# Attention over a paged cache: earlier key loads, value products moved within their slot, weights loaded in pieces, and a new first load of the condition weights

## The chip, the cores and the metric

The kernel runs on one core of a Trainium2 chip. The metric is the device time of the core in microseconds (us), from start to end of one execution; the time before is the median of three runs. A core has TensorE (PE, matrix products, into PSUM), VectorE (DVE), ScalarE (ACT), GpSimd (POOL) and SyncE (SP, which here only issues DMAs). Each takes its instructions in order and waits where an operand or a buffer isn't ready.

## The reference, cut to what matters

64 sequences of 32 tokens with 512 features. Each gets a 32x32 mixing matrix by its condition, then attention with 32 query heads and 8 key heads of 128 features over 512 cached keys, found by a block table, and its 32 new keys.

```python
W = weights[condition]                        # (64, 32, 32)
x = x + einsum('bct,bcd->bdt', x, W)
q = rope(rmsnorm(x @ Wq.T)); k = rope(rmsnorm(x @ Wk.T)); v = x @ Wv.T
kc = k_cache[block_table]; vc = v_cache[block_table]      # 16 pages of 32 rows
scores = einsum('bqhd,bkhd->bhqk', q, concat(kc, k)) * SCALE
scores = where(valid, scores, -1e30)          # a cached row counts below cache_seqlens
o = einsum('bhqk,bkhd->bqhd', softmax(scores), concat(vc, v))
x = x + o @ Wo.T
```

All is float32.

## The kernel before

The work is tiled by steps. A step is four sequences (called batches, 4 x 32 = 128 tokens) and half of the heads (4 key heads, 16 query heads); 16 steps (NT) do the first half of the heads, 16 more the second half, so there are 32. The first half also makes the mixed x and keeps it transposed in memory (`x1t_d`), and stores its part of the output (`acc_d`); the second half loads both again.

Inside a step the main loop goes over 4 batches (`bt`) and 4 key heads (`g`), 16 slots (`slot = bt * GH + g`). Each slot has the scores of one batch and head with its 512 cached keys (`scores`, L527, then the exponential on ScalarE, L535) and the value products of the slot before (`values`, L585). The rest of the work is put in certain slots:

- slot 0: `new_scores`, the scores of the step's new keys (`psn`, L545) and their exponential `pn`; and `x1_a` and `x1_c` of the next step. `x1_c` (L346) multiplies x with the block-diagonal tile `bd` of condition weights and VectorE adds the result to x (L347). In the second half `x1_a` only loads `acc` and `x1t`, and `x1_c` and `x1_b` do nothing.
- slot 1: `new_values(st, 0)`, the value products of the new keys for two heads: four PSUM tiles `pnv` (L569), one a batch, copied by ScalarE to `nv` (L577).
- slot 3: `x1_b` (transposes of the mixed x, L354), `out_proj` of the step before (L474, 32 passes, with VectorE's addition at L481), `new_values(st, 2)`, and in the first steps the angles of later steps (`angles`, L136 to L150).
- slots 4 to 13: projections of the next step (`k_a`, `q_a`, `v_a`), their norm and rotation on VectorE and ScalarE, and the transposes back (`k_b`, `q_b`).
- slots 5 and 6: the store of the step before, the load of x and of the condition weights of the step after next.

`values` of the second head of a pair ends with three VectorE operations: an addition into `nv` (L597), a reciprocal, and the product `o` (L600), which `turn` transposes into `ot` for the output projection. There is one `nv` buffer, so a step's first copies at L577 come after the last `o` of the step before.

Buffers: all PSUM tiles of projections, transposes, `psn`, `pmix`, `pnv` and `pout` share one pool of four (`ps_p`, tag `pp`); one `new_values` takes all four. The scores have two PSUM tiles, the values two.

Keys: `Batch(...)` asks for the keys of a batch (`load_k`, L279): 16 DMAs of 64 KB from SP, one a page, into one of two buffers `k_t`. A buffer is free again when the four copies `kh` (`head_keys`, L520; in the opening on ScalarE, L518) of its batch are made; in the loop they are made one batch ahead of their scores. The request for batch b + 2 stands at the end of batch b's four slots. Values: GpSimd gathers 128 rows at a time (`fetch`, L303) and ScalarE masks them into place (`fill`, L316), ordered behind the last instruction noted in `last["act"]`.

Weights: `load_w` loads 1 MB from SP. The output weights of the first half are loaded in slots 9 to 12 of step 0, those of the second half in slots 12 to 15 of step 16; the k, v and q weights of the second half in slots 11 to 13 of step 14.

The order of SP's and TensorE's instructions is as written; that of the other engines is made by a planner from estimated times, save in the opening (up to `opening.close()`), where all is in written order. DMAs from SP and ScalarE share eight completion semaphores in turn; a DMA waits for the one before it on the same semaphore.

The opening: ScalarE loads the conditions, reads them as registers and issues four loads of 4 KB into `bd`; SP loads x and the weights q 0, k, q 1, q 2 before the first batch's keys. Sixteen `warm` products keep TensorE busy first.

Of the kernel before, what the change touches and what calls it, by code (L numbers as in the profile page):

```python
# [11 lines left out]
F32 = mybir.dt.float32  # L12
# [7 lines left out]
P = 128  # L20
# [35 lines left out]
def cond_resid_paged_attention_kernel(  # L56
# [36 lines left out]
    cond_row = const.tile([1, NT, BT], I32, tag="cond", name="cond_row")  # L93
    lens_sb = const.tile([P, NT], I32, tag="lens", name="lens_sb")
# [90 lines left out]
    def steps_of(exact, pools):  # L185
# [37 lines left out]
        def load_w(kind, hh, g=0):  # L223
            if kind == "q":
                src = wq[:, (hh * QH + g * REP) * D : (hh * QH + (g + 1) * REP) * D]
            elif kind == "o":
                src = wo[(hh * QH + g * REP) * D : (hh * QH + (g + 1) * REP) * D, :]
            else:
                src = (wk if kind == "k" else wv)[:, hh * GH * D : (hh + 1) * GH * D]
            t = wpool.tile(  # L230
                [P, 4, 512], F32, tag=f"w{kind}{g}", name=f"w{kind}{g}_{hh}_{uid}"
            )
            wt[kind, hh, g] = t
            if kind == "o" and not exact:
                src = src.rearrange("(h j p) e -> h p j e", h=REP, p=S)
                for h in range(REP):
                    nc.sync.dma_start(t[h * S : (h + 1) * S, :, :], src[h])
                return
            nc.sync.dma_start(t, src.rearrange("(c p) e -> p c e", p=P))
# [315 lines left out]
        def new_values(st, g0):  # L555


            if g0 == 0:
                st.nv = work.tile(
                    [P, BT, GH, D + 1], F32, tag="nv", name=f"nv_{st.name}", bufs=1  # L560
                )
            pv = [
                ps_p.tile([P, 2, D + 1], F32, tag="pp", name=f"pnv_{st.name}_{g0}_{bt}")
                for bt in range(BT)
            ]
            for i in range(2):
                for bt in range(BT):
                    own = slice(bt * S, (bt + 1) * S)
                    nc.tensor.matmul(  # L569
                        pv[bt][:, i, :],  # L570
                        st.pn[own, g0 + i, :],
                        st.vn[own, g0 + i, :],
                        start=True,
                        stop=True,
                    )
            for bt in range(BT):
                nc.scalar.copy(st.nv[:, bt, g0 : g0 + 2, :], pv[bt])  # L577
# [94 lines left out]
        if not exact:  # L672
            nc.scalar.dma_start(cond_row, cond.rearrange("(i s) t -> s t i", s=S)[0:1])
            nc.gpsimd.dma_start(pages_sb, pages)
            nc.gpsimd.dma_start(norm_w["q"], qn_w.partition_broadcast(P))
            nc.gpsimd.dma_start(norm_w["k"], kn_w.partition_broadcast(P))
# [40 lines left out]
        load_cond_weights(0, nc.scalar, mybir.EngineType.Activation)  # L717
        load_w("k", 0)
        load_w("q", 0, 1)
        load_w("q", 0, 2)  # L720
        batch = Batch(first, 0)
# [17 lines left out]
        angles(0, trig)  # L739
        x1_a(first)  # L740
# [24 lines left out]
        scores(batch, 0)  # L765
        k_b(first)
# [36 lines left out]
        def pieces(st):  # L803
            do = {
                0: (x1_a, x1_c),
                3: (x1_b,),
# [13 lines left out]
        batch, later = later, Batch(first, 2)  # L820
# [13 lines left out]
        for st in steps:  # L834
# [4 lines left out]
            for bt in range(0 if st.n else 1, BT):  # L839
                this = batch  # L840
                for g in range(GH):
# [5 lines left out]
                    if slot == 1:  # L847
                        new_values(st, 0)
                    for piece in fill.get(slot, ()):
                        if isinstance(piece, tuple):  # L850
                            piece[0](ahead, piece[1])
                        else:
                            piece(ahead)
                    if slot == 3:
                        out_proj(steps[st.n - 1])
                        new_values(st, 2)
                        if st.n + 1 < NT // TRIG:
                            tmp = work.tile(
                                [P, 3, TRIG * HD], F32, tag="w1", name=f"trig_{st.n}"
                            )  # L860
# [7 lines left out]
                    if st.n == 0 and 9 <= slot < 13 or st.n == NT and slot >= 12:  # L868
                        load_w("o", st.hh, (slot - 9 if st.n == 0 else slot - 12))
                    if st.t == NT - 2 and st.hh + 1 < NHH:  # L870
                        if slot == 11:
                            load_w("k", st.hh + 1)
                            load_w("v", st.hh + 1)
                        if slot in (12, 13):
                            for i in range(2):
                                load_w("q", st.hh + 1, 2 * (slot - 12) + i)
# [3 lines left out]
                    if valued is not None:  # L880
                        values(*valued)
# [6 lines left out]
                batch, later = later, None  # L888
                n = st.n * BT + bt + 2
                if n < NHH * NT * BT:  # L890
                    later = Batch(steps[n // BT], n % BT)
                    unfilled += [(later, c) for c in range(VC)]
# [78 lines left out]
```

## Time and profile before

| | us |
|---|---|
| median of 3 runs (2278.62 to 2281.65) | 2279.99 |
| the profiled execution | 2282.54 |
| its span | 2280.7 |
| first output projection begins (step 1) | 120.53 |
| from one output projection to the next, first half (190.68 to 260.84) | 70.16 |
| the same, second half (1316.96 to 1385.91) | 68.95 |
| the same, from step 16 to 17 (1171.85 to 1248.10) | 76.25 |

In the slices of the page, TensorE's clock is at nine tenths or more throughout and the DMA engines are 70 to 80% busy in the first two slices (57 us each), 30 to 50% in most others. A matmul row of the timeline is a run of passes; float32 takes two passes a product, and the length of a pass is modelled, so the distance between starts tells more than the busy time. A projection of 8 passes takes 3.44 us, the output projection of 32 takes 13.75 us, the scores or values of one batch and head 0.89 us.

### The profile page before, as it was taken

Reading aid. Unit: us, or ns where it says so; the run is one execution under the profiler, and the core shown is the slowest. Engines: PE = TensorE matmul, PEld = TensorE weight load, DVE = VectorE, ACT = ScalarE, POOL = GpSimd, SP = SyncE. Lnnn points to the kernel's source line nnn. Section 1 sums busy time; section 2 is a strip of 40 time slices with the busy share of each in tenths; the row PEclk is TensorE's granted clock in tenths of the full one; section 3 lists DMA queues with packets and bytes.
Section 4 is the critical chain, followed back from the end, with each engine's and each line's share of the span. In section 5 each row is a group of like instructions: output and inputs, shape, how many; then the busy total and the mean of one; then the engine's idle time right before and its main releaser. Section 6 shows DMA issues by size and latency. Waiting matters only on the chain.

```text
span 2280.7 us, 41860 instructions
## 1 busy us (share of the span) xinstructions
PE 2233.9 (98%) x13590; PEld 1567.2 (69%) x13590; DVE 1075.5 (47%) x2717; ACT 943.2 (41%) x1726; POOL 772.5 (34%) x1005
## 2 busy tenths in 40 slices
PE   7999999999999999999999999999999999999998
PEld 5766677666776667766677766677666777666775
DVE  4544455544454444554444544445434455444452
ACT  3444444444443334443344334444333444333442
POOL 3423333323333233332333323333323343333331
PEclk9999999999999999999999999999999999999999
DMA  7844454344443444445657444544344554344442
GB/s 219 197 132 127 139 149 127 110 131 142 140 134 117 135 135 139 141 121 161 199 152 175 142 129 127 152 139 136 112 135 132 149 148 118 115 137 142 144 134 68
DMA packets 364486, 318.13 MB, mean 139 GB/s; under 512 B 46737, under 2 KB 308881, under 8 KB 364257
## 3 DMA queue, kind: packets, MB, share of 16 engines
q1 hardware_dynamic: 320064, 176.53, 27.1%
q0 software_dynamic: 41136, 134.55, 19.6%
q10 hardware_dynamic: 3056, 4.27, 0.5%
q8 instruction: 110, 1.80, 0.3%
q14 instruction: 120, 0.97, 0.1%
HBM read 302.59 MB, written 12.58 MB: 138 GB/s over the span
## 4 chain that ended last, share of the span: by engine, by line
PE 88%; DMA 5%; DVE 2%; SPq 2%; issue 1%; ACT 1%; another core or an unknown queue 0%; ACTq 0%; POOL 0%; DVEq 0%
PE pout_x L474 19%; PE po_x L585 18%; PE pp_q_x L390 18%; PE ps_x L527 17%; PE pp_v_x L390 5%; PE pp_k_x L390 5%; PE pt_q_x L434 2%; PE pnv_x L569 2%; DMA raw_x<-in_vc_dram,v_row 2%; SPq L279 1%; PE psn_x L545 1%; DMA wo_x<-in_wo_dram 1%; PE pmix_x L346 1%; DMA k_t_x<-in_kt_dram 1%; PE pt_k_x L434 1%
## 5 line engine op out<-in xcount | busy, mean ns | idle before, releaser
L303 POOL DMA_INDIRECT raw_x<-in_vc_dram,v_row x512 | 511.9, 1000 | 679.4 <-ACT v_x L316 612.0
L585 PE MATMUL po_x<-v_x,pr_x 128*128 128x129 f32 x4096 | 550.4, 277 | 3.7 <-ACT pr_x L535 3.7
L527 PE MATMUL ps_x<-qt_x,kh_x 128*128 128x128 f32 x4096 | 544.2, 276 | 6.9 <-DVE kh_x L520 4.6
L585 PEld LDWEIGHTS po_x<-v_x,pr_x 128*128 128x128 f32 x4096 | 504.6, 192 | 51.4 <-issue 38.4
L527 PEld LDWEIGHTS ps_x<-qt_x,kh_x 128*128 128x128 f32 x4096 | 500.9, 193 | 9.5 <-issue 6.8
L390 PE MATMUL pp_q_x<-wq_x,x1t_x 128*128 128x512 f32 x1024 | 460.6, 592 | 0.0
L535 ACT ACTIVATE pr_x<-ps_x 128x512 f32<-128x512 f32 x512 | 304.8, 600 | 376.3 <-PE ps_x L527 325.4
L474 PE MATMUL pout_x<-wo_x,ot_x 128*128 128x512 f32 x1024 | 445.7, 593 | 1.6 <-ACT nv_x L577 1.3
L316 ACT ACTIVATE v_x<-raw_x,valid 128x512 f32<-128x512 f32 x512 | 361.6, 720 | 115.2 <-DMA raw_x<-in_vc_dram,v_row 112.4
L474 PEld LDWEIGHTS pout_x<-wo_x,ot_x 128*128 128x128 f32 x1024 | 192.0, 190 | 231.9 <-issue 228.9
L390 PEld LDWEIGHTS pp_q_x<-wq_x,x1t_x 128*128 128x128 f32 x1024 | 187.2, 190 | 198.5 <-issue 198.2
L520 DVE COPY kh_x<-k_t_x 128x512 f32<-128x512 f32 x506 | 215.3, 428 | 201.4 <-PE ps_x L527 102.2
L577 ACT COPY nv_x<-pnv_x 128x258 f32<-128x258 f32 x256 | 77.3, 389 | 337.2 <-PE pnv_x L569 274.3
L400 ACT ACTIVATE sq_q_x<-pp_q_x 128x512 f32<-128x512 f32 x128 | 76.4, 597 | 299.0 <-issue 133.1
L404 DVE TENSOR_REDUCE ms_q_x<-sq_q_x 128x4 f32<-128x512 f32 x128 | 87.2, 681 | 199.2 <-ACT sq_q_x L400 199.2
L407 POOL TENSOR_TENSOR rs_q_x<-ms_q_x,minus_half 128x4 f32<-128x4 f32 x128 | 132.4, 1035 | 129.6 <-DVE ms_q_x L405 129.5
L379 POOL TENSOR_TENSOR cw_k_x<-norm_k,cos 128x64 f32<-128x64 f32 x32 | 10.1, 315 | 440.3 <-DVE ms_k_x L405 440.3
L597 DVE TENSOR_TENSOR nv_x<-po_x,nv_x 128x258 f32<-128x258 f32 x256 | 107.2, 419 | 104.9 <-PE po_x L585 52.9
L411 DVE TENSOR_TENSOR rope_q_x<-pp_q_x,cw_q_x 128x512 f32<-128x512 f32 x128 | 87.3, 682 | 102.6 <-PE pt_k_x L434 102.6
L390 PE MATMUL pp_v_x<-wv_x,x1t_x 128*128 128x512 f32 x256 | 115.2, 593 | 0.2 <-DMA wv_x<-in_wv_dram 0.2
L390 PE MATMUL pp_k_x<-wk_x,x1t_x 128*128 128x512 f32 x256 | 115.2, 592 | 0.0
L600 DVE TENSOR_TENSOR o_x<-nv_x,rden 128x256 f32<-128x256 f32 x256 | 107.5, 420 | 3.3
(95 smaller groups left out, 1426.0 us busy)
## 6 DMA issues: line engine op xcount, KB each, us to landing
k_t_x<-in_kt_dram SPq DMA_DIRECT2D x2048, 64.0 KB
wq_x<-in_wq_dram SPq DMA_DIRECT2D x8, 1024.0 KB
raw_x<-in_vc_dram,v_row POOLq DMA_INDIRECT x512, 4.3
wo_x<-in_wo_dram SPq DMA_DIRECT2D x32, 256.0 KB
xt_x<-in_x_dram SPq DMA_DIRECT2D x16, 256.0 KB
x1t_d<-x1t_x ACTq DMA_DIRECT2D x16, 256.0 KB
acc_d<-xt_x SPq DMA_DIRECT2D x16, 256.0 KB
acc_x<-acc_d SPq DMA_DIRECT2D x16, 256.0 KB
```

What stands on the lines that cost most here:

```text
L303: nc.gpsimd.indirect_dma_start(out=raw.rearrange("p g d -> p (g d)"), out_offset=None, in_=vc, in_offset=bass.IndirectOffsetOnAxis(ap=v_ro ...
L316: nc.scalar.activation(v_bufs[b % 2][:, c, :, 0:D], raw, AF.Copy, scale=ok)
L390: nc.tensor.matmul(pp, st.x1t[:, c, :], w[:, c, :], start=(c == 0), stop=(c == KC - 1))
L407: nc.gpsimd.tensor_tensor(rs, ms, minus_half, ALU.pow)
L411: nc.vector.tensor_tensor(r.rearrange("p h e f -> p h (e f)"), pp.rearrange("p (h d) -> p h d", h=4), cw.rearrange("p e f -> p (e f)").uns ...
L474: nc.tensor.matmul(po, st.ot[:, i, :], wt["o", st.hh, i // 4][:, i % 4, :], start=(i == 0), stop=(i == QH - 1),)
L520: last["dve"] = nc.vector.tensor_copy(k, ba.k_raw[:, :, g, :]).ins
L527: nc.tensor.matmul(ps[:, c, :], ba.k[g][:, c * P : (c + 1) * P], queries(ba, g), start=True, stop=True,)
L535: last["act"] = nc.scalar.activation(pr, ps, AF.Exp, scale=SCALE).ins
L585: nc.tensor.matmul(ba.po[:, g % 2, :], ba.pr[g][:, c, :], ba.v_t[:, c, g, :], start=(c == 0), stop=(c == VC - 1),)
L597: nc.vector.tensor_tensor(t, ba.po, t, ALU.add)
L600: nc.vector.tensor_tensor(ba.o[:, both, :], t[:, :, 0:D], rd.unsqueeze(2).to_broadcast([P, 2, D]), ALU.mult,)
```

## The change

Five edits. The request for keys moves to the start of a batch's slots. In slots 0 to 3 `values` comes ahead of the pieces; `new_values(st, 2)` stands behind the scores of slot 3, ahead of `values`, `x1_b` and `out_proj`; `x1_c` moves from slot 0 to slot 2; `new_values` notes its last copy in `last["act"]`, behind which `fill` and the angles are ordered. Weights are loaded in halves (`load_parts`), over slots 4 to 11 of steps 0 and 16 and over 12 slots of steps 14 and 15. In the opening the condition weights of step 0 come by one gather of GpSimd and four VectorE copies, and k and q 1 are loaded by GpSimd behind it, the keys ahead of q 2.

```diff
-        def load_w(kind, hh, g=0):
+        def load_w(kind, hh, g=0, part=slice(0, 4), eng=nc.sync):
...
+            if part.start == 0:
+                wt[kind, hh, g] = wpool.tile(
+                    [P, 4, 512], F32, tag=f"w{kind}{g}", name=f"w{kind}{g}_{hh}_{uid}"
+                )
+            t = wt[kind, hh, g]
             if kind == "o" and not exact:
                 src = src.rearrange("(h j p) e -> h p j e", h=REP, p=S)
-                for h in range(REP):
+                for h in range(part.start, part.stop):
                     nc.sync.dma_start(t[h * S : (h + 1) * S, :, :], src[h])
                 return
-            nc.sync.dma_start(t, src.rearrange("(c p) e -> p c e", p=P))
+            eng.dma_start(t[:, part, :], src.rearrange("(c p) e -> p c e", p=P)[:, part, :])
+
+        def load_parts(which, hh, at):
+
+            if 0 <= at < 2 * len(which):
+                load_w(which[at // 2][0], hh, which[at // 2][1], slice(at % 2 * 2, at % 2 * 2 + 2))
...
-                nc.scalar.copy(st.nv[:, bt, g0 : g0 + 2, :], pv[bt])
+                last["act"] = nc.scalar.copy(st.nv[:, bt, g0 : g0 + 2, :], pv[bt]).ins
...
-            nc.scalar.dma_start(cond_row, cond.rearrange("(i s) t -> s t i", s=S)[0:1])
+            nc.scalar.dma_start(cond_0, cond[:, 0:1])
+            nc.vector.tensor_scalar(cond_0, cond_0, float(S), row, ALU.mult, ALU.add)
...
-        load_cond_weights(0, nc.scalar, mybir.EngineType.Activation)
-        load_w("k", 0)
-        load_w("q", 0, 1)
+        w_sel = work.tile([P, S], F32, tag="o", name="w_sel", bufs=1)
+        nc.gpsimd.indirect_dma_start(
+            out=w_sel,
+            out_offset=None,
+            in_=w_cond,
+            in_offset=bass.IndirectOffsetOnAxis(ap=cond_0, axis=0),
+        )
+        nc.scalar.dma_start(cond_row, cond.rearrange("(i s) t -> s t i", s=S)[0:1])
+        load_w("k", 0, eng=nc.gpsimd)
+        load_w("q", 0, 1, eng=nc.gpsimd)
+        batch = Batch(first, 0)
         load_w("q", 0, 2)
-        batch = Batch(first, 0)
...
         angles(0, trig)
+        for i in range(BT):
+            blk = slice(i * S, (i + 1) * S)
+            nc.vector.tensor_copy(bd[blk, blk], w_sel[blk, :])
         x1_a(first)
...
         scores(batch, 0)
+        after = Batch(first, 2)
...
-                0: (x1_a, x1_c),
-                3: (x1_b,),
+                0: (x1_a,),
...
-        batch, later = later, Batch(first, 2)
+        batch, later = later, after
...
             for bt in range(0 if st.n else 1, BT):
-                this = batch
+                this, after = batch, None
+                n = st.n * BT + bt + 2
+                if n < NHH * NT * BT:
+                    after = Batch(steps[n // BT], n % BT)
+                    unfilled += [(after, c) for c in range(VC)]
...
-                    if slot == 1:
-                        new_values(st, 0)
+                    if slot in (1, 3):
+                        new_values(st, slot - 1)
+                    if slot < GH and valued is not None:
+                        values(*valued)
...
+                    if slot == 2 and ahead:
+                        x1_c(ahead)
                     if slot == 3:
+                        if ahead:
+                            x1_b(ahead)
                         out_proj(steps[st.n - 1])
-                        new_values(st, 2)
...
-                    if st.n == 0 and 9 <= slot < 13 or st.n == NT and slot >= 12:
-                        load_w("o", st.hh, (slot - 9 if st.n == 0 else slot - 12))
-                    if st.t == NT - 2 and st.hh + 1 < NHH:
-                        if slot == 11:
-                            load_w("k", st.hh + 1)
-                            load_w("v", st.hh + 1)
-                        if slot in (12, 13):
-                            for i in range(2):
-                                load_w("q", st.hh + 1, 2 * (slot - 12) + i)
+                    if st.t == 0:
+                        load_parts([("o", i) for i in range(GH)], st.hh, slot - GH)
+                    if st.n in (NT - 2, NT - 1):
+                        load_parts(
+                            [("k", 0), ("q", 0), ("q", 1), ("v", 0), ("q", 2), ("q", 3)],
+                            1,
+                            slot - 5 + (st.n - NT + 2) * BT * GH,
+                        )
...
-                    if valued is not None:
+                    if slot >= GH and valued is not None:
                         values(*valued)
...
-                batch, later = later, None
-                n = st.n * BT + bt + 2
-                if n < NHH * NT * BT:
-                    later = Batch(steps[n // BT], n % BT)
-                    unfilled += [(later, c) for c in range(VC)]
+                batch, later = later, after
```

More of the change, by code (lines that the diff above doesn't have):

```diff
@@ L93, in cond_resid_paged_attention_kernel @@
     cond_row = const.tile([1, NT, BT], I32, tag="cond", name="cond_row")
+    cond_0 = const.tile([P, 1], I32, tag="cond_0", name="cond_0")
     lens_sb = const.tile([P, NT], I32, tag="lens", name="lens_sb")
@@ L229, in load_w @@
                 src = (wk if kind == "k" else wv)[:, hh * GH * D : (hh + 1) * GH * D]
[L230 to L233, printed above, removed]
+            if part.start == 0:
[3 more added lines that the diff above has]
+            t = wt[kind, hh, g]
             if kind == "o" and not exact:
                 src = src.rearrange("(h j p) e -> h p j e", h=REP, p=S)
-                for h in range(REP):
+                for h in range(part.start, part.stop):
                     nc.sync.dma_start(t[h * S : (h + 1) * S, :, :], src[h])
                 return
-            nc.sync.dma_start(t, src.rearrange("(c p) e -> p c e", p=P))
+            eng.dma_start(t[:, part, :], src.rearrange("(c p) e -> p c e", p=P)[:, part, :])
+        def load_parts(which, hh, at):
+            if 0 <= at < 2 * len(which):
+                load_w(which[at // 2][0], hh, which[at // 2][1], slice(at % 2 * 2, at % 2 * 2 + 2))
         def load_cond_weights(t, eng=nc.sync, kind=mybir.EngineType.SP):
@@ L853, in steps_of @@
                             piece(ahead)
+                    if slot == 2 and ahead:
+                        x1_c(ahead)
                     if slot == 3:
+                        if ahead:
+                            x1_b(ahead)
                         out_proj(steps[st.n - 1])
-                        new_values(st, 2)
                         if st.n + 1 < NT // TRIG:
-                            tmp = work.tile(
-                                [P, 3, TRIG * HD], F32, tag="w1", name=f"trig_{st.n}"
-                            )
+                            tmp = work.tile([P, 3, TRIG * HD], F32, tag="w1", name=f"trig_{st.n}")
                             with tc.issue_after(last["dve"]), tc.issue_after(last["act"]):
```

## The prediction

> **What bounds the kernel now.** I read the page's busy times first, then TensorE's waits, then the timeline of TensorE over a few steps, then the other engines at the places where it stops.
>
> ```profile
> PE 2233.9 (98%) x13590; PEld 1567.2 (69%) x13590; DVE 1075.5 (47%) x2717; ACT 943.2 (41%) x1726; POOL 772.5 (34%) x1005
> ...
> PE pmix_x L346 <- DMA bd<-in_w_cond_dram: 8.6, 1, 8.6
> PE pnv_x L569 <- DVE xt_x L481: 5.7, 16, 0.4
> PE pnv_x L569 <- DVE acc_x L481: 5.4, 15, 0.4
> PE ps_x L527 <- DVE kh_x L520: 4.6, 1, 4.6
> PE po_x L585 <- ACT pr_x L535: 3.7, 1, 3.7
> ```
>
> TensorE is the bound: 2280.7 - 2233.9 = 46.8 us of the span are not matmul, so no reordering can bring more than that plus what is lost to a slow clock. The wait view (waiter, releaser: total us, times, longest) names four places: the opening, a hole in each of the 31 steps after the first, and two single stops. In the timeline (start us, length us, engine, line, tiles, idle before):
>
> ```profile
> 1798.37 0.73 PE L569 MATMUL pnv_x<-vn_x,pn_x 32*128 32x129 f32 x16
> 1799.03 1.16 PE L585 MATMUL po_x<-v_x,pr_x 128*128 128x129 f32 x8
> ...
> 1816.54 0.50 PE L569 MATMUL pnv_x<-vn_x,pn_x 32*128 32x129 f32 x6
> 1817.39 0.71 PE L569 MATMUL pnv_x<-vn_x,pn_x 32*128 32x129 f32 x10 [0.36 <-DVE acc_x L481]
> 1818.03 1.16 PE L585 MATMUL po_x<-v_x,pr_x 128*128 128x129 f32 x8
> ```
>
> The first half of the new keys' value products takes 1799.03 - 1798.37 = 0.66 us, the second half 1818.03 - 1816.54 = 1.49 us: three products (six passes) run, the fourth waits until the output projection has left the PSUM tile that it needs. That is 0.83 us a step, 31 x 0.83 = 25.7 us, more than the wait view shows (11.1), since pipelined ends are counted busy.
>
> The stops at step changes:
>
> ```profile
> 103.10 1.06 PE L585 MATMUL po_x<-v_x,pr_x 128*128 128x129 f32 x8
> 108.72 2.05 PE L527 MATMUL ps_x<-qt_x,kh_x 128*128 128x128 f32 x8 [4.57 <-DVE kh_x L520]
> ...
> 1233.22 1.08 PE L545 MATMUL psn_x<-qt_x,kn_x 128*32 128x128 f32 x32
> 1237.98 1.16 PE L585 MATMUL po_x<-v_x,pr_x 128*128 128x129 f32 x8 [3.68 <-ACT pr_x L535]
> ```
>
> Both follow the loads of the output weights, 4 MB in a few slots. What else matters is in slots 0 to 3 of an ordinary step:
>
> ```profile
> 749.24 0.43 DVE L520 COPY kh_x<-k_t_x 128x512 f32<-128x512 f32 x1 [2.73 <-DMA k_t_x<-in_kt_dram]
> ...
> 750.23 0.43 DVE L600 TENSOR_TENSOR o_x<-nv_x,rden 128x256 f32<-128x256 f32 x1
> ...
> 750.75 1.21 ACT L577 COPY nv_x<-pnv_x 128x258 f32<-128x258 f32 x4 [2.21 <-DVE o_x L600]
> ...
> SPq L279 <- DVE kh_x L520: 449.6, 60, 11.9
> ```
>
> VectorE stands 2.73 us at a key copy whose keys have not landed; behind it stands the end of the last step's `o_x`, and behind that ScalarE's four copies that empty the first `pnv` tiles, 3.26 us after these products began (747.49). Today nothing on TensorE needs those tiles for a while. The last line says that SP's key loads wait for a free key buffer, not for their place in the queue.
>
> **What the Trainium skill says.** "Perfetto Trace Analysis", Optimizing Tensor Performance, Matmuls: independent groups should rotate through PSUM banks so that emptying one overlaps the next; the trace agrees, and the hole above is this rotation running out (four tiles, all taken by one `new_values`). "TensorE: Matmul & The Clock Gate", HAM oscillation: a TensorE idle for about 3.4 us falls to half clock; here, after 4.57 us, eight score passes take 2.05 us in place of 1.06. "DMA: Bandwidth & Descriptors", Issuing engines are not separate DMA queues: transfers of all queues run on the same 16 engines and interleave; the trace shows the effect, since loads of 8 KB (`lens_sb`) and 4 KB (`bd`) beside the first weights take 5.93 and 8.86 us on the chain of waits. The same page, Anatomy of one DMA, gives about 2.0 us fixed for a GpSimd DMA; the 256 KB gathers here take 4.3 us (median).
>
> **The change, part by part**, against the profiled execution (2282.5 us, span 2280.7; 2.5 above the median).
>
> *Second half of the value products first in slot 3.* Removes the hole: -25.7. It no longer waits for the projection, but for the four copies of the first half, only 7 to 8 us of TensorE work earlier in place of 18. The copies come as late as the keys. In steps with x still to be mixed (first half), `x1_c` moves from slot 0 to slot 2 and needs one of those tiles too, and the second half then needs the tile that VectorE's addition after `x1_c` frees. Worked out from the score product of new keys (`psn`) as zero: the late key copy starts at 5.24 us on average in steps 7 to 14, `o_x` ends 0.97 later, ScalarE's first copy begins at 6.3, and is done after 0.39, the third after 0.93. `x1_c` would be ready at 6.45 (1.01 + 0.99 + 0.99 + 0.66 + 1.0 + 0.89 + 0.9), starts at 6.75 to 7.3: wait 0.3 to 0.85, I take 0.6. The addition behind two key copies, the transpose and the next `o_x` ends near 9.1, about when it is needed: 0.1. So 0.7 in 8 steps: +5.6. In steps 3 to 6 the changed order puts five operations of the angle table (0.23 to 0.29 us each) ahead of that addition, and keys land at 5.6: 1.85 in 4 steps, +7.4. In steps 1, 2, 15 and 17 no late key copy precedes `o_x`, or no mix is left: 0. In the second half (15 steps, no mix): copies from 6.57 to 7.8, the products ready at 7.33 wait 0.27 for the fourth tile; ScalarE's exponentials come after the copies, so the next value products wait some 0.2 more and the projection up to 0.3, against about 0.3 that it waits today: 0.45 net, +6.8. With the mix gone from slot 0, `pn` has 0.9 us less cover in 14 steps, as the second half has today (2.4 us of such waits in the trace): +2. Together -25.7 + 21.8 = -3.9. Ends: the waits could sum to 5 (early tile, keys early) or 40 (last tile, additions late).
>
> *Keys asked for a batch sooner.* The request leaves its place behind the store, the x load and the condition weights (slots 5, 6), so only the fourth batch's keys start about 20 us sooner; they were not late. The batch that stops VectorE in slot 0 is bound by its buffer: copy at 735.78, first load 736.42, 16 loads over some 9 us, landed at 749.24. That stays. In the second half the `acc` and `x1t` loads now stand behind 16 key loads (about 9 us), needed 24 us after slot 0: 0. SP stays behind no new wait: 0, ends -3 and +3.
>
> *Weights in pieces.* Output weights go from slots 9 to 12 of step 0 to slots 4 to 11 as halves, so the keys of step 1 stand behind 2 MB that are done earlier, not 3 MB. The stop at 108.72 should go: 4.57, and the slow clock after it (scores to projection 120.36 - 108.72 = 11.64 against 9.60 elsewhere: 2.0), so -6.6 (ends -3, -7.5). In step 16, 4 MB in slots 12 to 15 become halves in slots 4 to 11; the stop in step 17 costs 1248.10 - 1171.85 = 76.25 us against 68.9 for a neighbour, 7.3; half of the bytes still stand before late keys, I take -5 (0, -7.3). The k, v, q loads of the second half are spread over 12 slots: the 0.85 us wait at 1098 shrinks, -0.5. Cover gone, each would cost what it does now.
>
> *First gather.* The mix waits until 16.61 for condition weights. Now: 512 bytes of indices, one VectorE operation, one gather of 16 KB (issue 1 us, 2 to 4.3 us to land), four small copies that stand behind the angle operations (they end at 13.67 today, since `freq` lands at 11.6). So the mix could start at 10 to 14.2, 2.4 to 6.6 us sooner. But SP's remaining key loads in the opening wait behind ScalarE's DMA of x1t and the four condition loads, on shared semaphores, and wq 2, wv and wq 3 follow those; they would be issued near 23 us, so the third q projection or v becomes late instead. I take -2.5 (ends +1, -7).
>
> Sum: -3.9 - 6.6 - 5.0 - 0.5 - 2.5 = -18.5. 2280.0 - 18.5 = 2261.5.
>
> **Rivals.** *A, the steps gain too*: the tile that `x1_c` gets is free in time, new waits are 0.15 us a step. For it: four tiles and 7 us of cover; against it: the copies at 750.75 lie after the point where `x1_c` would stand. -25.7 + 4.7 - 14.6 = -35.6: 2244. *B, slower*: one mechanism, ScalarE's late first copies. If `x1_c` gets the last tile and the second half waits for an addition behind everything VectorE has queued, a step pays 1.8 us on average, 31 x 1.8 = 56: -25.7 + 56 - 14.6 = +15.5, 2296. It decides from (25.7 + 14.6 + 4.6) / 31 = 1.45 us a step on. For it: VectorE does stand at the keys in nearly all steps; against it: `o_x` to first copy is only 0.09 us, and my sum gives 0.7. *C, the loads only move*: the gains of weights and opening return as late keys (DMA is 70 to 80% busy in the first slices). -3.9 alone: 2276.
>
> **How the numbers follow.** Forecast 0.54, A 0.26, B 0.12, C 0.08. A measurement of this kernel tells 0.2% (4.6 us) from no change. C is half faster, half same; the forecast's own spread puts 0.02 into same. Faster 0.82, same 0.06, slower 0.12. Range 2242 to 2277: from A's gain to C; B is left out with the rest of the tails.
>
> **What would show it.** Right: the wait of `pnv` on the projection's additions is gone, `pmix` and `pnv` wait for ScalarE's `nv` copies or VectorE's addition in the first half, 0.3 to 2 us each, the key copy in slot 0 still waits 2 to 3 us, steps 1 and 17 take 70 us or less to the projection, the first mix starts at 10 to 14 us. Wrong: key copies that no longer wait (then A), waits above 1.45 us a step (B), new stops of 3 us or more behind weight loads (C).

## The result and the profile after

The changed kernel takes 2260.25 us (median of 5 runs, 2257.33 to 2266.80) against 2280.14 us (5 runs, 2278.62 to 2282.26): ratio 0.9916, 95% interval 0.9897 to 0.9935, 19.9 us faster. The profiled execution took 2258.59 us, 23.95 less than the profiled one before. The forecast was 2261.5.

The page's busy times and, below them, the wait view of the kernel after, VectorE's line and then TensorE's (waiter, releaser: total us, times, longest):

```profile
PE 2223.5 (99%) x13590; PEld 1565.7 (69%) x13590; DVE 1076.0 (48%) x2722; ACT 940.4 (42%) x1724; POOL 779.8 (35%) x1008
```

```profile
DVE kh_x L527 <- DMA k_t_x<-in_kt_dram: 68.2, 34, 3.7
```

```profile
PE po_x L592 <- ACT pr_x L542: 5.6, 3, 3.0
PE pp_q_x L397 <- ACT qt_x L469: 3.3, 1, 3.3
PE pmix_x L353 <- DVE bd L757: 2.8, 1, 2.8
...
PE pmix_x L353 <- ACT nv_x L584: 2.2, 3, 1.2
```

TensorE's idle time fell from 46.8 to 2256.8 - 2223.5 = 33.3 us; the other 10 us of the gain were inside what the page counts as busy, as the ends of pipelined products are. The 31 waits of `pnv` on the projection's additions are gone. The late keys are still there: VectorE waits for them 34 times.

The timeline of TensorE in a step of the second half (step 20), from the score product of new keys to the projection:

```profile
1436.05 1.08 PE L552 MATMUL psn_x<-qt_x,kn_x 128*32 128x128 f32 x32
...
1439.05 0.73 PE L576 MATMUL pnv_x<-vn_x,pn_x 32*128 32x129 f32 x16
...
1443.47 0.87 PE L576 MATMUL pnv_x<-vn_x,pn_x 32*128 32x129 f32 x16
...
1445.27 11.32 PE L481 MATMUL pout_x<-wo_x,ot_x 128*128 128x512 f32 x26
```

Both halves of the value products now run through: 0.73 us, and 0.87 with a short pause inside. The same view in the first half (step 3), where x is mixed between them:

```profile
255.17 1.12 PE L353 MATMUL pmix_x<-xt_x,bd 128*128 128x512 f32 x2 [0.53 <-ACT nv_x L584]
256.13 1.05 PE L534 MATMUL ps_x<-qt_x,kh_x 128*128 128x128 f32 x8
257.11 0.50 PE L576 MATMUL pnv_x<-vn_x,pn_x 32*128 32x129 f32 x6
258.49 0.71 PE L576 MATMUL pnv_x<-vn_x,pn_x 32*128 32x129 f32 x10 [0.87 <-DVE xt_x L354]
```

Here are the two new waits of the prediction: the mix behind ScalarE's copy, the fourth value product behind VectorE's addition.

And the chain of waits of the kernel after at step 1, where a stop was forecast to go (start us, length us):

```profile
96.05 9.96 DMA raw_x<-in_vc_dram,v_row
106.06 0.60 issue
106.66 0.58 ACT pr_x L542
...
107.29 1.51 PE po_x L592 x8
```

The stop is still there, and another wait ends it: a gather of values takes 9.96 us from issue to landing, beside the output weights in SP's queue:

```profile
79.56 12.20 SPq L286 DMA_DIRECT2D k_t_x<-in_kt_dram  x16
91.81 5.74 SPq L239 DMA_DIRECT2D wo_x<-in_wo_dram  x8
```

The pieces of slots 8 to 11 stood behind a key request that waited for its buffer until 91.76 us, and then came out as one bunch of 2 MB. Pieces in the program were not pieces in the queue.

The starts of `psn` step by step give the ledger (kernel after less kernel before, in the two profiled executions, us):

| stretch | predicted | measured |
|---|---|---|
| opening, to step 0 | -2.5 | -3.5 |
| step 0 to 2 (output weights, one hole) | -7.4 | +0.3 |
| step 2 to 15 (13 steps, x mixed) | +4.1 | -1.2 |
| step 15 to 18 (weights of the second half) | -7.5 | -5.5 |
| step 18 to 31 (13 steps, no mix) | -4.9 | -13.1 |
| step 31 to end | -0.4 | -0.9 |

Predicted rows are the terms on record, spread over the steps they speak of (one hole of 0.83 beside the -6.6 in the second, 13 of -0.83 + 13.0 + 1.9 in the third, 13 of -0.83 + 0.45 in the fifth). The sum came out; three rows are wrong: the second by 7.7 us one way, the third and the fifth by 5.3 and 8.2 us the other. The pair of profiles differs by 4 us more than the medians do, so a row is not exact. The question for the runs was whether the parts act alone, why the second half gained so much more, and what holds the stop at step 1.

### The profile page after: what moved, and what is told of

Its sections match the earlier page's. It is cut to its first block, busy times and chain, and to the rows that moved or that the text cites. A ratio compares the mean times of both kernels' runs of the same rounds, so it can differ in the third digit from the quotient of the medians.

```text
span 2256.8 us, 41920 instructions
## 1 busy us (share of the span) xinstructions
PE 2223.5 (99%) x13590; PEld 1565.7 (69%) x13590; DVE 1076.0 (48%) x2722; ACT 940.4 (42%) x1724; POOL 779.8 (35%) x1008
## 4 chain that ended last, share of the span: by engine, by line
PE 90%; DMA 4%; DVE 2%; issue 2%; SPq 2%; ACT 1%; POOL 1%; ACTq 0%; DVEq 0%; POOLq 0%
PE pout_x L481 19%; PE pp_q_x L397 19%; PE po_x L592 18%; PE ps_x L534 18%; PE pp_k_x L397 5%; PE pp_v_x L397 5%; PE pt_q_x L441 2%; PE pnv_x L576 2%; DMA raw_x<-in_vc_dram,v_row 2%; SPq L286 1%; PE psn_x L552 1%; DMA k_t_x<-in_kt_dram 1%; PE pt_k_x L441 1%; PE pmix_x L353 1%; DMA pages_at<-in_pages_v_dram 0%
## 5 line engine op out<-in xcount | busy, mean ns | idle before, releaser
L488 DVE TENSOR_TENSOR xt_x<-pout_x,xt_x 128x512 f32<-128x512 f32 x16 | 11.1, 692 | 246.6 <-PE pout_x L481 246.6
L488 DVE TENSOR_TENSOR acc_x<-pout_x,acc_x 128x512 f32<-128x512 f32 x16 | 11.1, 692 | 220.7 <-PE pout_x L481 220.7
```

## The experiments

The kernel before was run beside each group; its median went from 2278.7 to 2283.6 us between groups, so ratios are compared.

### Each part alone

**Slot order (p1).** The edit to the kernel before, with `new_values` noting its last copy as in the change, cut:

```diff
-                0: (x1_a, x1_c),
-                3: (x1_b,),
+                0: (x1_a,),
...
-                    if slot == 1:
-                        new_values(st, 0)
+                    if slot in (1, 3):
+                        new_values(st, slot - 1)
+                    if slot < GH and valued is not None:
+                        values(*valued)
...
+                    if slot == 2 and ahead:
+                        x1_c(ahead)
                     if slot == 3:
+                        if ahead:
+                            x1_b(ahead)
                         out_proj(steps[st.n - 1])
-                        new_values(st, 2)
```

> The kernel before with the slot order alone (second half of the value products first in slot 3, x1_c in slot 2, x1_b in slot 3, value products of slots 0 to 3 ahead of the other pieces). Theory S, the slot order by itself earned what the steps gained in the trace after (2.9 us over steps 2 to 16 and 13.1 us over steps 18 to 31): -14 to -17 us against before, second-half periods at 68.0 to 68.3 us. Rival K, the waits that I charged are real and the earlier key requests removed them: -4 us (my prediction of this part), second-half periods near 68.9 us with waits of pnv on the nv copies of 0.3 us and more.

2274.35 us, ratio 0.9963 (0.9954 to 0.9972), -8.4 us. Its 20 runs spread from 2265.5 to 2280.3; the profiled one is at 2270.96. In that trace the second half gains 13.15 us from step 18 to 31, just what the whole change gains there, with periods of 68.0 to 68.5 us and a few longer ones: theory S holds for the second half, K falls. For the first half S gave -2.9 us, and steps 2 to 15 lose 1.7 us. The last step takes 3.6 us more than before, with a stop of 2.27 us at a key copy. So the time gained less than S gave.

**Keys sooner (p2).**

```diff
-                this = batch
+                this, after = batch, None
+                n = st.n * BT + bt + 2
+                if n < NHH * NT * BT:
+                    after = Batch(steps[n // BT], n % BT)
...
-                batch, later = later, None
+                batch, later = later, after
```

> The kernel before with only the key requests a batch sooner. Theory S and my prediction: 0 us, within 1. Rival K in its strong form (keys sooner shorten every step): -3 us or more, and the key copy of slot 0 starts earlier than 5.2 us after the score product of new keys. If the acc and x1t loads of the second half suffer behind the key loads: +1 to +3 us in steps 17 to 31.

2302.59 us, ratio 1.0081 (1.0055 to 1.0107): 18.5 us slower, which no theory had. The timeline of SP and of TensorE in this kernel:

```profile
66.38 23.55 SPq L279 DMA_DIRECT2D k_t_x<-in_kt_dram  x32
89.98 12.86 SPq L237 DMA_DIRECT2D wo_x<-in_wo_dram  x12
104.12 22.85 SPq L279 DMA_DIRECT2D k_t_x<-in_kt_dram  x16
127.02 1.94 SPq L237 DMA_DIRECT2D wo_x<-in_wo_dram  x4
```

```profile
117.05 10.46 PE L474 MATMUL pout_x<-wo_x,ot_x 128*128 128x512 f32 x24
134.43 6.14 PE L474 MATMUL pout_x<-wo_x,ot_x 128*128 128x512 f32 x8 [6.91 <-DMA wo_x<-in_wo_dram]
```

The last quarter of the output weights stood behind 16 key loads that waited for a buffer until 127 us, and the projection waited 6.91 us for it. Three such stops (13.4 us in the wait view, one in step 1 and two in step 17), one of 4.21 us ahead of the first k projection of the second half, and slow passes after them (8 of the projection take 6.14 us, 24 before them 10.46) make the loss: step 1 to 2 takes 83.67 us in place of 71.20, step 15 to 16 76.14 in place of 69.78, step 17 to 18 82.13 in place of 76.25. Step 0 to 1 is shorter, 44.92 us in place of 50.51. From step 2 to 15 the periods are as before; from step 18 to 31 they sum to 1.6 us more.

**Weights in pieces (p3).**

```diff
-                    if st.n == 0 and 9 <= slot < 13 or st.n == NT and slot >= 12:
-                        load_w("o", st.hh, (slot - 9 if st.n == 0 else slot - 12))
+                    if st.t == 0:
+                        load_parts([("o", i) for i in range(GH)], st.hh, slot - GH)
```

(and `load_parts` for the k, q and v weights, as in the change)

> The kernel before with only the loads of the weights in pieces. My prediction: -12 us (step 0 to 1 -6.6, step 16 to 17 -5.0, step 15 -0.5). Rival C, the stop only moves: as in the trace after, about 0 at step 1 (a late gather beside the output weights instead of late keys) and -3.7 at step 17, -4 us in all. If the new stop of step 1 in the trace after came from the earlier key requests and not from the pieces, the step 0 to 1 period falls to 72 us or less here and the sum is -8 us or better.

2279.15 us, ratio 0.9991 (0.9980 to 1.0003), -2.0 us, with an interval that reaches no change. Step 17 to 18 takes 70.15 us in place of 76.25: that term is right (-6.1). Steps 0 to 2 take 120.6 us in place of 121.7: the stop only moved, to 100.72 us. From its chain of waits:

```profile
81.53 11.77 DMA wo_x<-in_wo_dram
...
96.13 3.13 DMA k_t_x<-in_kt_dram
...
100.72 2.05 PE ps_x L533 x8
```

SP's key loads wait here for the end of an output weight load that takes 11.77 us, and the scores for the late keys. That is not the stop of the kernel after, which a gather ends. So pieces alone don't remove a stop, as rival C says, but whether the one at step 1 depends on the earlier key requests is not told by this run. After an idle time of only 2.29 us TensorE's clock was 0.62 from 100 to 102 us, and eight passes took 2.05 us: a slow clock doesn't need the 3.4 us that the prediction names.

**Opening (p4).**

```diff
-        load_cond_weights(0, nc.scalar, mybir.EngineType.Activation)
-        load_w("k", 0)
-        load_w("q", 0, 1)
-        load_w("q", 0, 2)
-        batch = Batch(first, 0)
+        w_sel = work.tile([P, S], F32, tag="o", name="w_sel", bufs=1)
+        nc.gpsimd.indirect_dma_start(
...
+        load_w("k", 0, eng=nc.gpsimd)
+        load_w("q", 0, 1, eng=nc.gpsimd)
+        batch = Batch(first, 0)
+        load_w("q", 0, 2)
```

> The kernel before with only the opening changed (indices and one gather for the first condition weights, wk and the second wq on GpSimd's queue, cond_row later). My prediction: -2.5 us. The trace after: -3.5 us at the score product of new keys of step 0; the rival is that this head start is lost to late keys or gathers at step 1, because the output weights then meet the same loads: 0 us at the end.

2281.19 us, ratio 0.9990 (0.9978 to 1.0001), -2.3 us; step 0 starts 1.9 us sooner and 2.1 us of it are left at step 14. The size is as predicted, but the interval reaches no change.

The four parts sum to +5.8 us, the change to -19.9: they don't add. The second run suggests which pair interacts: earlier key requests do harm while whole weights stand behind them.

### One part taken out, or moved

**The change without the earlier keys (q1).**

```diff
-                this, after = batch, None
-                n = st.n * BT + bt + 2
-                if n < NHH * NT * BT:
-                    after = Batch(steps[n // BT], n % BT)
-                    unfilled += [(after, c) for c in range(VC)]
+                this = batch
```

(the request goes back to the end of the batch)

> The kernel after with only the key requests back at the end of a batch. The kernel before with the earlier requests alone became 18.5 us slower, since the weights stand behind them in SP's queue. Theory N, with the weights in pieces the earlier requests give nothing (my prediction, 0): within 2 us of the kernel after, some 2260 us, ratio to before 0.991 to 0.992. Theory K, once the pieces are there the earlier requests earn the rest (the sum of the four single parts is +6 us, the change as a whole -19): 8 to 14 us slower than the kernel after, ratio 0.995 to 0.998; step 0 to 1 then takes 49 to 50 us, not 46.6.

2265.78 us, ratio 0.9928 (0.9901 to 0.9955) against 0.9916 (0.9897 to 0.9935) of the whole change: no difference that these runs can tell. Step 0 to 1 does take 50.8 us, not 46.6, but step 1 to 2 then takes 69.5 and not 75.5. Given the other parts, the earlier requests earn about nothing: theory N. The three other parts sum to -12.7 us alone, and this run has -16.4, so most of what doesn't add comes with the key requests. That it is the pieces that keep these from costing 18.5 us is read from the trace of p2; the two were not run together without the rest.

**Half of the first output weights in the opening (q2)**, the rest every second slot.

```diff
         later = Batch(first, 1)
+        load_w("o", 0, 0)
+        load_w("o", 0, 1)
...
-                    if st.t == 0:
+                    if st.n == 0 and slot % 2 == 0:
+                        load_parts([("o", 2), ("o", 3)], st.hh, (slot - GH) // 2)
+                    if st.n == NT:
                         load_parts([("o", i) for i in range(GH)], st.hh, slot - GH)
```

> The kernel after with the first two heads of the first output weights (2 MB) asked for in the opening, behind the second batch's keys, the other two in halves in slots 4, 6, 8 and 10. Theory D, the stop at step 1 is transfer bandwidth (share of the DMA engines 0.94 to 0.98 from 80 to 110 us, 0.44 from 40 to 60 us): steps 0 to 2 take 117 us or less in place of 122.0, ratio to before 0.989 to 0.990. Rival O, it is the order on SP (pieces bunched behind a request that waits for its buffer): the pieces left over still bunch and the stop stays, 121 to 123 us. Rival L, the 2 MB delay q, v and the first gathers in the opening by 2 to 8 us: step 0 starts later by that much and nothing is gained.

2258.60 us, ratio 0.9889 (0.9872 to 0.9905). Steps 0 to 2 take 46.48 + 70.49 = 116.97 us in place of 122.03, the size that theory D gave; step 0 starts 1.9 us later (rival L, in part), and steps 2 to 15 take 3.6 us more than in the kernel after. The view of stretches shows the bytes moved (start:end, length, busy times, clock, DMA share, GB/s). The kernel after:

```profile
40.00:60.00 20.00, 19.39 (x130) 12.33 (x130) 8.77 (x18) 8.52 (x16) 8.47 (x15) 1.00 0.44 128
...
80.00:100.00 20.00, 20.00 (x136) 16.08 (x136) 12.33 (x32) 10.50 (x19) 10.66 (x15) 1.00 0.96 231
```

and this one:

```profile
40.00:60.00 20.00, 19.38 (x112) 11.63 (x111) 9.39 (x19) 10.08 (x19) 9.12 (x15) 1.00 0.79 184
...
80.00:100.00 20.00, 18.98 (x125) 15.03 (x125) 12.93 (x35) 9.60 (x18) 10.65 (x14) 1.00 0.95 223
```

From 80 to 100 us the engines are as full as before, so fullness alone doesn't stop TensorE; what changed is how many weight loads SP issues at once (bunches of four, not eight) and how many fall into these steps. Total and bunching were changed together, and these runs don't separate them.

**The mix back in slot 0 (q3).**

```diff
-                0: (x1_a,),
+                0: (x1_a, x1_c),
...
-                    if slot == 2 and ahead:
-                        x1_c(ahead)
```

> The kernel after with only x1_c back in slot 0, where the kernel before has it; the second half of the value products stays first in slot 3. My prediction put 0.7 to 1.85 us a step of the first half on the tile that x1_c takes in slot 2 (mix behind the nv copies, value products behind the addition). If that term is right, the waits of pmix on nv and of pnv on xt go, and the first-half steps fall from 69.3 to 71.5 us to about 69.4 us: 3 to 8 us faster than the kernel after. Rival: the first value products then find no fourth tile until the addition behind the late keys is done, as in slot 3 of the kernel before: no gain, or a loss of 0.5 us and more in each of 14 steps (+7 us).

2288.31 us, ratio 1.0034 (1.0018 to 1.0050): slower than before the change. The wait view of this kernel, and its timeline in step 7:

```profile
PE pnv_x L576 <- DVE xt_x L354: 20.4, 12, 3.0
```

```profile
536.99 1.02 PE L353 MATMUL pmix_x<-xt_x,bd 128*128 128x512 f32 x2
537.85 1.05 PE L534 MATMUL ps_x<-qt_x,kh_x 128*128 128x128 f32 x8
538.83 0.50 PE L576 MATMUL pnv_x<-vn_x,pn_x 32*128 32x129 f32 x6
542.37 0.71 PE L576 MATMUL pnv_x<-vn_x,pn_x 32*128 32x129 f32 x10 [3.04 <-DVE xt_x L354]
```

The first value products wait for the addition: 1.7 us in each of 12 steps, and steps 2 to 15 take 26 us more than in the kernel after. The main theory of the expectation is wrong, the rival too low. The kernel before mixes in slot 0 too, reaches these products at the same 3.85 us after `psn`, and pays nothing. VectorE's timeline shows why, here:

```profile
541.22 0.43 DVE L527 COPY kh_x<-k_t_x 128x512 f32<-128x512 f32 x1 [3.61 <-DMA k_t_x<-in_kt_dram]
541.57 0.16 DVE L606 RECIPROCAL rden<-nv_x 128x2 f32<-128x2 f32 x1
541.64 0.67 DVE L354 TENSOR_TENSOR xt_x<-pmix_x,xt_x 128x512 f32<-128x512 f32 x1
```

and in the kernel before:

```profile
535.35 0.69 DVE L347 TENSOR_TENSOR xt_x<-pmix_x,xt_x 128x512 f32<-128x512 f32 x1 [3.31 <-PE pmix_x L346]
538.85 0.43 DVE L520 COPY kh_x<-k_t_x 128x512 f32<-128x512 f32 x1 [2.81 <-DMA k_t_x<-in_kt_dram]
```

Since the change emits the value products of slots 0 to 3 ahead of the other pieces, the addition has come to stand behind the late key copy; before, it stood ahead of it. So this run changed two things, and the loss belongs to the place on VectorE's queue. It shows what a place behind the late keys costs, not that slot 0 is bad for the mix.

**The page table first, the second condition weights on SP (q4).**

```diff
+        nc.gpsimd.dma_start(pages_at, pages_v)
...
         load_w("k", 0, eng=nc.gpsimd)
...
-        load_cond_weights(1, nc.scalar, mybir.EngineType.Activation)
+        load_cond_weights(1)
```

> The kernel after with the page and length tables on GpSimd's queue ahead of wk and the second wq, and the condition weights of step 1 on SP in place of ScalarE. If the 8.8 us that the page table takes behind the two weights, and the 6.2 us that ScalarE stands at the condition weights, are what loses the head start (first mix 6.5 us sooner, step 0 only 3.5 us): step 0 starts at 53 to 55 us in place of 56.7, 2 to 4 us faster than the kernel after. Rival: weights then land 0.5 to 1 us later and the q projections wait for these, step 0 within 1 us of 56.7.

2266.70 us, ratio 0.9931 (0.9914 to 0.9948), and step 0 starts 6.4 us later than in the kernel after. The chain of waits shows which half of the edit did it. On SP the small loads came behind the second batch's keys (issued at 40.57 us), and the second mix waited 6.8 us. The first score product had been reached at 32.31 us in place of 34.20, so the page table may be worth its place; the two edits should have been two runs.

### Toward a better version

**The mix behind the value products (s1).** The mix in slot 2 is what still takes a tile between the two halves, so it goes behind them, and the transposes into the projection at three quarters:

```diff
-                    if slot == 2 and ahead:
-                        x1_c(ahead)
                     if slot == 3:
                         if ahead:
-                            x1_b(ahead)
-                        out_proj(steps[st.n - 1])
+                            x1_c(ahead)
+                        out_proj(steps[st.n - 1], ahead and (lambda: x1_b(ahead)))
```

> The kernel after with x1_c moved from slot 2 to slot 3, behind the second half of the value products and ahead of the output projection, and x1_b to three quarters of that projection. Theory T, what the first half still loses is the tile that x1_c takes between the two halves of the value products: the waits of pmix on nv and of pnv on xt go, the first-half steps take 69.3 to 69.6 us each, and steps 2 to 15 take 902 to 905 us in place of 911.3: 6 to 9 us faster than the kernel after, ratio to before 0.987 to 0.989. Rival V, the losses come from VectorE's late keys and angle operations, wherever the mix stands: the addition or the copy of x1t is late for the k projection in slot 4, steps stay at 70 us and more.

2258.94 us, ratio 0.9921 (0.9904 to 0.9937): no faster than the kernel after, yet theory T holds step by step. Steps 2 to 15 take 903.7 us in place of 911.3, most periods are 69.32 us, and the waits on `xt` are gone. The place of the mix and that of the transposes were changed together. The gain is given back in step 1 to 2, 81.97 us in place of 75.47. The chain there:

```profile
127.86 0.45 PE px1t_x L361 x4
128.33 0.59 ACT x1t_x L363
128.95 2.06 DMA x1t_d<-x1t_x
131.02 0.33 SPq L286
```

SP's next key load is released by the end of ScalarE's store of `x1t`. The later transposes make this store later, the keys later, and TensorE waits 6.50 us for a key copy.

**With the earlier output weights (s2).**

> As s1, and 2 MB of the first output weights asked for in the opening, as in q2. If the two gains add: steps 0 to 2 again 117 us in place of 122, 4 to 5 us faster than s1 less up to 2 us in the opening; ratio to before 0.985 to 0.987. Rival: the earlier weights only move late keys into the following steps, same time as s1 within 1 us.

The edits of s1 and q2 together: 2245.51 us (2242.13 to 2249.13), ratio 0.9857 (0.9839 to 0.9875): the fastest, 32.6 us below before and some 13 us below the change. Steps 0 to 2 take 115.3 us, 13.2 less than in s1 where 4 to 5 were expected, since the stop of step 1 to 2 is gone too; steps 2 to 15 take 904.8. The timeline of step 8:

```profile
597.56 1.09 PE L576 MATMUL pnv_x<-vn_x,pn_x 32*128 32x129 f32 x16
...
599.58 1.02 PE L353 MATMUL pmix_x<-xt_x,bd 128*128 128x512 f32 x2
600.44 10.46 PE L481 MATMUL pout_x<-wo_x,ot_x 128*128 128x512 f32 x24
610.74 0.60 PE L361 MATMUL px1t_x<-ident,xt_x 128*128 128x128 f32 x4
```

**The second half's output weights ahead of the key requests (s3)**, added to s2; the loads in slots 4 to 11 of step 16 go.

```diff
+                if st.n == NT:
+                    for at in range(3 * bt - 4, 3 * bt - 1):
+                        load_parts([("o", i) for i in range(GH)], st.hh, at)
                 this, after = batch, None
```

> As s2, and in step 16 the eight halves of the output weights are asked for ahead of the key requests of the second, third and fourth batch (two, three, three) in place of one in each of slots 4 to 11. If what steps 16 and 17 lose is the bunch of weight loads beside a gather: periods 16 to 17 and 17 to 18 fall from 70.7 and 70.9 us to 68.0 to 69 us, 3 to 5 us faster than s2. Rival, bandwidth in these steps is short anyway, or keys become late behind the three loads of the fourth batch: no change, or a new stop in step 17.

2245.82 us, ratio 0.9859 (0.9843 to 0.9876): as the last one, without the 3 to 5 us expected. Steps 16 to 18 take 138.1 in place of 138.9 us. Most of what these steps lost in the kernel after (141.5) was already gone in the last run.

**The third wq ahead of the first keys (s4)**, added to s3.

```diff
-        batch = Batch(first, 0)
         load_w("q", 0, 2)
+        batch = Batch(first, 0)
```

> As s3, and in the opening the third wq is asked for ahead of the first batch's 16 key loads, not behind them (the changed kernel issues it at 20.6 us; the third q projection waits 3.3 us and then runs at half clock). If the order on SP is the reason: that projection starts near 25.7 us, step 0 some 3 to 5 us sooner than s3. Rival: the same bytes earlier delay wk, the second wq or the page table, and the projections before it wait 2 to 4 us instead: no gain.

2248.55 us, ratio 0.9869 (0.9852 to 0.9885). The third q projection follows without a wait, but the first mix starts at 13.95 us, not at 10.27, and the first q projection at 20.08, not at 15.54; step 0 starts 0.8 us sooner and nothing is left of it. That is the rival: in the opening each load that comes sooner makes another one late.

## Why the prediction was right or wrong

**The sum** was right within 1.3 us of the median, in good part by luck: terms cancelled. The weights at step 1 gave 7.7 us less, the steps of the first half 5.3 us more, those of the second 8.2 us more.

**The hole** was real and goes: the slot order alone gives steps of 68.02 us, which is 68.86, about the shortest of before, less 0.83 (within 0.01).

**First half, right in mechanism, too high in two terms.** "So 0.7 in 8 steps", "1.85 in 4 steps". Against 69.32 us (70.15 less 0.83, the period that s1 reaches), the slot order alone pays 0.72 us in steps 7 to 14 and 1.68 in steps 3 to 6; in the whole change it is 0.68 and 1.18. With the mix behind the value products most steps reach that floor (0.11 and 0.42 above it), so its place costs; that it does so by the tile is what the two waits shown for step 3 say. The term "+2" for less cover of `pn` didn't come: the floor leaves nothing for it, and TensorE's wait view of these steps in the kernel after has no wait for `pn`. These two make 4.6 us of the row's 5.3; most of the rest is one longer step of before (70.66).

**Second half, mis-sized.** The term is "0.45 net, +6.8"; measured, it is about -0.18 a step. It summed new waits of 0.27, 0.2 and up to 0.3 and took off "about 0.3 that it waits today". In the kernel before the projection stands where the value products stand now and needs the first of the same tiles. From the start of the first value products to the projection takes 4.33 us at best and 4.53 on average: 0.20 us of that wait, so the old part was not too small. The new one is 0.25 us, not 0.77: this is the figure that failed. The three waits were added, and measured they come to about one of them. So moving the wait cost 0.05 us, since the same copies were waited for already. Another 0.19 us is a gain that the term doesn't have: ahead of the first value products the kernel before lost 0.28 us on average, the kernel after 0.09. Two lines of the wait view of the kernel before, in its second half, show both kinds:

```profile
PE pnv_x L569 <- ACT pn_x L553: 1.3, 3, 0.5
PE pout_x L474 <- ACT nv_x L577: 1.3, 4, 0.6
```

Single traces scatter here. Over the four kernels with the old order the copies cost 0.20 to 0.48 us a step, over the ten with the new order 0.21 to 0.58. All losses together, above the shortest step, are 0.51 to 0.86 (mean 0.68) and 0.33 to 0.68 (mean 0.50). So the term is near zero or a little below, not +0.45; why less is lost ahead of the first value products stays open.

**Keys sooner, right by luck of company.** "SP stays behind no new wait: 0". In this change that is what q1 shows. Alone it is false by 18.5 us: what stands behind a key request on SP is the output weights, and I named the `acc` and `x1t` loads only.

**Weights in pieces: the step that failed** is "The stop at 108.72 should go: 4.57, and the slow clock after it ..., so -6.6". It counted bytes by slot ("halves ... in slots 4 to 11") and not by place in SP's queue. The pieces of slots 8 to 11 came out together at 91.81 us, behind keys waiting for a buffer, and a gather on GpSimd's queue beside them took 9.96 us. Steps 0 to 2 lost 0.3 us with the hole's 0.83 in it, in place of gaining 7.4. That the bunch made the gather late is the reading of the chain; q2, where the stop is gone, changed the bunch and the bytes together. The Trainium skill, "DMA: Bandwidth & Descriptors", Issuing engines are not separate DMA queues, says that queues share the same engines; I used it for the opening and not here; the 9.96 us against 4.3 of a usual gather (median of the kernel before) agree with it. In step 17 the term was about right: -6.1 alone, -5.4 in the change with the hole in it, for -5.0; but step 16 to 17 lost 1.7 us in the change.

**Opening, about right** in size (-2.5; -3.5 in the trace, -2.3 timed alone with an interval that reaches no change) and in what is late next: the third q projection, at 29.00 us, after a wait of 3.3. The first mix starts at 10.12 us.

**Rivals.** A's condition (0.15 us a step of new waits) was not met; the second half gained more than A gives it all the same (1.01 us a step for 0.68), since most of its new wait replaced an old one and less was lost ahead of it. B's mechanism, an addition behind everything that VectorE has queued, is real: q3 shows it at 1.7 us a step, where the mix holds a tile and its addition stands behind the late keys. The change put the mix late enough to escape most of it. C, its gain lost again to another stop, is what happened at step 1.

## What to carry to other kernels

Place a load by its position in the issuing queue, not by its place in the program: behind a request that waits for a buffer, pieces become one bunch again, and an earlier request can hold back everything that follows it. When a wait is moved, measure how long its place was waiting already, for the same release: only the difference is new (0.05 us here, of 0.25). Parts of a change can depend on each other (one of these costs 18.5 us without its partner), so take one out of the whole as well as trying each alone.

## What was not expected of the hardware

- Where SP's key loads follow a store issued by ScalarE, they can be released by its end: the longest such wait of SP for an `x1t` store is 19.3 us in the kernel after and 21.6 in s1. With the store's end at 131.0 us and not 123.4, TensorE stopped for 6.5 us.
- Runs of one kernel on one chip can spread widely: 20 runs of the slot order alone cover 14.8 us, 39 runs of the kernel before 10 us, four runs of s3 2.0 us. An effect of 2 us in one trace (a step longer by 1 to 2 us here and there) is not a finding.
- In the kernel after, the 256 KB gathers issued between 88 and 110 us whose landing is recorded take 3.4 to 5.6 us; the one beside eight weight loads takes 9.96.
